# Making part of a scan's inputs on TensorE in the last layer of a four-layer network

## The chip, the cores and the metric

The kernel runs on one NeuronCore of a Trainium2 chip. The metric is the device time of one execution in microseconds, and the whole computation is in fp32. Five engines work side by side, each through its own instruction stream in order: TensorE (PE in the profile, its weight loads PEld), VectorE (DVE), ScalarE (ACT), GpSimd (POOL) and SyncE (SP), which here issues the DMAs.

## The reference

Four layers follow one another on an image batch; all of them hold selective state-space scans. Only the last one is touched. It normalises the image, runs one bidirectional Mamba over the rows and one over the columns, joins them with a linear map, and ends in an MLP. What its scans compute:

```python
def _mamba(x, W_in, conv_w, conv_b, W_x, W_dt, b_dt, A_log, D, W_out):
    xz = jnp.einsum('nld,ed->nle', x, W_in)
    xi, z = (xz[..., :di], xz[..., di:])                 # di = 384
    xp = jnp.pad(xi, ((0, 0), (K - 1, 0), (0, 0)))       # K = 4 taps
    xc = conv_b + sum((xp[:, k:k + L, :] * conv_w[:, k] for k in range(K)))
    xc = _silu(xc)
    dbc = jnp.einsum('nld,ed->nle', xc, W_x)
    dt = jax.nn.softplus(jnp.einsum('nlr,dr->nld', dbc[..., :dr], W_dt) + b_dt)
    Bm = dbc[..., dr:dr + ds]                            # ds = 16 states
    Cm = dbc[..., dr + ds:]
    A = -jnp.exp(A_log)
    def step(h, inp):
        dt_t, B_t, C_t, x_t = inp
        h = jnp.exp(dt_t[:, :, None] * A) * h + (dt_t * x_t)[:, :, None] * B_t[:, None, :]
        return (h, jnp.einsum('nds,ns->nd', h, C_t))
    ...
    y = jnp.swapaxes(ys, 0, 1) + D * xc
    y = y * _silu(z)
    return jnp.einsum('nld,od->nlo', y, W_out)

y1 = _mamba(xs, *p)
y2 = jnp.flip(_mamba(jnp.flip(xs, 1), *p), 1)            # the same weights, backwards
```

The images are 4 x 48 x 48 with 192 channels. In the last layer each row (or column) of 48 tokens is a sequence of its own.

## The kernel before

`network` runs layer 0, the inputs of layer 1, the scans of layers 1 and 2, then `row_mambas` for the last layer, then `mlp`. `row_mambas` makes a list of jobs. A job is one chunk of 384 tokens (eight sequences of 48) in one direction; the backward job of a chunk is the twin of the forward one and shares its projected input `xh` and its gate `z`. There are two sets of weights, four images, six chunks and two directions, so 96 jobs. In a job the 384 inner channels stand as three blocks `i` of 128 partitions, and the 16 states as four groups `g` of four (NG). A step of `run_jobs` handles one (job, i, g): 12 steps a job, 1152 in the layer.

In one step, VectorE (`scan`) first waits on an empty instruction for everything that the step needs, then multiplies du (delta times x, held in PSUM by `enter`) by the four rows of B, which `fetch` has spread over all partitions in `bcb`, into the PSUM tile `inputs`; then one scan instruction runs over all 4 x 384 elements with the decays `a` and writes `h`. The decay is zero at the first token of each sequence, so one scan passes over many sequences. ScalarE (`decay`) makes the four exps of a later step (`ahead` is 2), with three buffers of `a`. GpSimd (`weigh`) multiplies `h` by the four rows of C. TensorE (`reduce`) sums the states by identity matmuls into the PSUM tile `y`, which also takes D times x (`skip`, `diagD`). `take` copies `y` to SBUF on ScalarE, `gate` multiplies it by z on GpSimd. `h` has four buffers.

Beside the steps, `Stream` runs the projections of the next job as units, each with a slot in which TensorE begins it and one in which ScalarE evacuates it: `inner` (input projection), `conv` (the convolution, four matmuls with 128x128 diagonal weights `diag` for each of the three blocks), `bc` (B, C and the rank of delta; it also writes B and C to DRAM, from where `fetch` spreads them), `delta` (three of them), the z `gate` and the output projections. All of these use the two buffers of the PSUM tile `ps`. No unit is made more than two ahead of the last evacuated one. The order of a step's work on each engine is written out by hand in the loop of `run_jobs` and kept in program order on VectorE, GpSimd, TensorE and ScalarE.

[...]before, `y` takes two, `ps` two, `inputs` three and `du` one.

Of the kernel before, what the change touches and what calls it, by code (L numbers as in the profile page):

```python
# [14 lines left out]
ALU = mybir.AluOpType  # L15
# [3 lines left out]
S = 48  # L19
# [5 lines left out]
NCH = L // CH  # L25
N = 16
NG = 4

# [28 lines left out]
class K:  # L59
# [3 lines left out]
    def __init__(self, tc, ctx):  # L63
        self.tc, self.nc = tc, tc.nc
        self.v, self.g, self.t = (
            InOrder(tc, e) for e in (tc.nc.vector, tc.nc.gpsimd, tc.nc.tensor)
        )
        self.count = 0
        self.last_act = None
        self.table = None  # L70
        self.const = ctx.enter_context(tc.tile_pool(name="const", bufs=1))
        self.ident = self.tile(self.const, [128, 128], "ident")
        make_identity(self.nc, self.ident)

    def tile(self, pool, shape, tag, bufs=None):
        self.count += 1
# [161 lines left out]
class ScanPools:  # L238
# [6 lines left out]
    def __init__(self, k, ctx, parts, rows):  # L245
        pool = k.tc.tile_pool
        self.parts, self.rows = parts, rows
        self.wide = 128 // parts
        self.n = N // parts
        self.groups = self.n // NG  # L250
        self.W = W = CH if rows else CH + 1
        self.one = ctx.enter_context(pool(name="one", bufs=1))
        self.two = ctx.enter_context(pool(name="two", bufs=2))
        self.bcs = ctx.enter_context(pool(name="bcs", bufs=5 if rows else 4))
        self.hbufs = 4 if rows or parts == 2 else 3
        self.hs = ctx.enter_context(pool(name="hs", bufs=self.hbufs))
        self.y = ctx.enter_context(pool(name="y", bufs=2 if rows else 1, space=PSUM))
        self.ps = ctx.enter_context(pool(name="ps", bufs=2, space=PSUM))
        self.vec = ctx.enter_context(pool(name="vec", bufs=1, space=PSUM))

        inputs = k.tile(self.vec, [128, 1536 if rows else 2048], "inputs")
        self.b = inputs[:, : NG * W].rearrange("p (j l) -> p j l", l=W)
        self.du = k.tile(self.vec, [128, 512], "du")[:, :W]
        self.ones = k.tile(self.one, [128, 1], "ones")
        k.nc.vector.memset(self.ones, 1.0)
        self.decays = [k.tile(self.one, [128, NG, W], f"a{i}") for i in range(3)]
        self.n_decays = 0

        self.readers = []
        self.weighed = []  # L270
        self.n_h = 0
        self.entered = None
        self.revs = [None] * 3
        self.yts = 3 if rows else 2
        self.rev = None

        self.sum = k.ident
        if parts == 2:
            self.sum = k.tile(self.one, [128, 64], "sum")
            k.nc.vector.tensor_tensor(self.sum, k.ident[:, :64], k.ident[:, 64:], ALU.add)  # L280
# [28 lines left out]
class ScanJob:  # L309
# [10 lines left out]
    def close(self, i):  # L320
        pass

    def __init__(self, k, pools, w, c0, rev, prev):
        self.k, self.pools, self.w, self.c0, self.rev, self.prev = k, pools, w, c0, rev, prev
        self.entry, self.tokens = pools.entry(rev)
        self.bcb = {}
        self.fetched = {}
        self.y = {}
        self.a = {}
        self.h = {}  # L330
        self.du = {}

        self.waits = {}

# [12 lines left out]
    def projections(self, xs, *slots):  # L347

        k, nc, w, pools = self.k, self.k.nc, self.w, self.pools
        nr = 2 * N + w.rank  # L350
        W = pools.W

        def bc(px):
            self.bcd = k.tile(pools.two, [nr, W], "bcd", 1)
            if self.entry is not None:
                k.g.memset(self.bcd[:, self.entry : self.entry + 1], 0.0)
            k.copy(self.bcd[:, self.tokens], px)
            self.bc = k.dram([2 * N, W], "bc")
            nc.sync.dma_start(self.bc, self.bcd[: 2 * N, :])

        def delta(i):
            def act(pd):
                if i == 0:
                    self.delta = k.tile(pools.two, [128, 3, CH], "delta")
                k.act(self.delta[:, i, :], pd, AF.Softplus, bias=w.dtb[:, i, :])

            return self.unit(
                slots[1],
                128,
                lambda ps: (ps, [(w.dtT[2 * N : nr, i, :], self.bcd[2 * N : nr, self.tokens])]),  # L370
                act,
            )

        first = self.unit(
            slots[0],
            nr,
            lambda ps: (ps, [(w.xpT[:, i, :], xs()[: pools.wide, i, :]) for i in range(3)]),
            bc,
        )
        return first, [delta(i) for i in range(3)]  # L380

    def fetch(self, g):

# [45 lines left out]
    def enter(self, i):  # L429

        self.pools.turn(self.k, self.rev)
        self.pools.entered = self.k.copy(self.pools.du[:, self.tokens], self.du.pop(i))

    def scan(self, i, g):

# [282 lines left out]
        return units  # L718


class Stream:


# [62 lines left out]
def run_jobs(jobs, side=None):  # L786
# [1 line left out]

    ahead, behind, taken, gated, driven = 2, 1, 2, 3, 3
    last_group = jobs[0].pools.groups - 1
    groups = [(job, i, g) for job in jobs for i in range(3) for g in range(last_group + 1)]
    per = len(groups) // len(jobs)
# [14 lines left out]
    for t in range(driven):  # L809
        if first := at_group(t, 0):  # L810
            first[0].drive(first[1])
    jobs[0].enter(0)
    for job, i, g in groups[:ahead]:
        job.decay(i, g)
    stream = Stream([])
    for t in range(len(groups) + gated + 1):
        n, at = divmod(t, per)
# [5 lines left out]
        if at == per - ahead:  # L823
            stream.run(at - 1)
        if at == taken + 3 and n + 1 == len(jobs) and n:
            Stream(jobs[n - 1].outputs(*[(0, 0)] * 3)).run(per)
        if t < len(groups):
            job, i, g = groups[t]
            job.scan(i, g)
# [8 lines left out]
        if t < len(groups):  # L838
            if t + 1 < len(groups):
                job, i, g = groups[t + 1]  # L840
                job.carry(i, g)
            job, i, g = groups[t]
            job.weigh(i, g)
        stream.run(at if at < per - 1 else per)
        if t < len(groups):
            for slot, extra in jobs[n].extras:
                if slot == at:
                    extra()
# [9 lines left out]
        if 0 <= t - behind < len(groups):  # L858
            job, i, g = groups[t - behind]
            job.reduce(i, g)  # L860
    Stream(jobs[-1].outputs(*[(0, 0)] * 3)).run(per)
    offer(jobs[-1])


# [34 lines left out]
class MambaWeights(Weights):  # L899
    def __init__(self, k, pool, inT, xpT, dtT, vec, tag):  # L900
        super().__init__(k, pool, 128, 12, xpT, dtT, vec, tag)
        self.k, self.pool, self.in_src = k, pool, inT
        self.D = self.vec[:, :, 17:18]
        self.cb = self.vec[:, :, 18:19]
        self.taps = vec.shape[1] - 19
        self.diagD = k.tile(pool, [128, 3, 128], f"diagD{tag}")
        self.diag = k.tile(pool, [128, 3, self.taps, 128], f"diag{tag}")

    def scaled(self, out, by):
        self.k.nc.vector.tensor_scalar(out, self.k.ident, by, None, ALU.mult)  # L910

    def diagonals(self, i):

        self.scaled(self.diagD[:, i, :], self.D[:, i, :])
        for t in range(self.taps):
            self.scaled(self.diag[:, i, t, :], self.vec[:, i, 19 + t : 20 + t])

    def derive(self):

# [10 lines left out]
class PairWeights(MambaWeights):  # L930
# [15 lines left out]
        k.act(self.A, self.vec[:, :, 1 : 1 + N], AF.Exp)  # L946
        k.act(self.A, self.A, AF.Copy, scale=-1.0)

    def scaled(self, out, by):
        if not self.late:  # L950
            return super().scaled(out, by)
        self.k.act(out, self.k.ident, AF.Identity, scale=by)

    def extras(self):

# [632 lines left out]
def row_mambas(k, weights, sets):  # L1588
# [3 lines left out]
    with ExitStack() as ctx:  # L1592
        pools = ScanPools(k, ctx, 1, True)
        jobs = []
        for (there, back), (srcs, outs, prior) in zip(weights.pairs, sets):
            if jobs:

                jobs[-2].extras = [(1, there.enter)]
            for b in range(B):
                for c in range(NCH):  # L1600
                    of = None, srcs[b], outs[b]
                    last = prior[b] if prior is not None else None
                    first = MambaJob(k, pools, there, c * CH, False, *of)
                    jobs += [
                        first,
                        MambaJob(k, pools, back, c * CH, True, *of, twin=first, prior=last),
                    ]
        run_jobs(jobs)

# [170 lines left out]
    return np.concatenate([a if a.ndim == parts[-1].ndim else a[..., None] for a in parts], -1)  # L1780


def scan_rows(w, rank):

    bc = w[..., rank:, :]
    shape = bc.shape
    bc = bc.reshape(*shape[:-2], 2, N // NG, NG, shape[-1])
    bc = np.swapaxes(bc, -4, -3).reshape(shape)
    return swapped(np.concatenate([bc, w[..., :rank, :]], -2))


def mamba_layout(in_w, conv_w, conv_b, x_w, dt_w, dt_b, a_log, d):
    return {
        "inT": swapped(in_w),
        "xpT": scan_rows(x_w, 12),
        "dtT": swapped(dt_w),
        "vec": columns(dt_b, a_log, d, conv_b, conv_w),
    }


def layout(i):
# [50 lines left out]
    for p in ("mh", "mv"):  # L1852
        add(
            f"L3_{p}",
            **mamba_layout(
                *of(f"L3_conv_{p}", "Win", "convw", "convb", "Wx", "Wdt", "bdt", "Alog", "D")
            ),
            Wout=i[f"L3_conv_{p}_Wout"],
        )
    add(  # L1860
        "L3",
# [24 lines left out]
```

## Time and profile before

| what | value |
|---|---|
| median of 3 runs | 19325.0 us (19319.56 to 19327.51) |
| profiled execution, its own time | 19328.76 us |
| span in the profile | 19327.0 us |
| mean granted TensorE clock | 0.907 |
| VectorE busy | 18079.9 us, 94% |
| TensorE matmul busy | 16851.2 us, 87% |
| GpSimd busy | 14748.4 us, 76% |
| ScalarE busy | 13012.9 us, 67% |
| the last layer's steps | first multiply at 12872.84 us, last scan ends at 18869.98 us |

A row of the profile names a group of instructions by line, engine, operation, output and inputs, with its count, busy time, the mean of one in ns and the idle time of the engine before it. Line 56 is the helper that keeps program order, line 93 the helper of ScalarE's activations, so groups are told apart by the names of their tiles. An fp32 matmul stands as two MATMUL and two LDWEIGHTS records. A busy time of PE covers overlapping records once.

### The profile page before, as it was taken

How to read it: one execution, taken by the hardware profiler on the slowest of the kernel's cores; microseconds unless marked ns; L12 is line 12 of the kernel's file. 1: busy time of each engine (PE TensorE's matmuls, PEld its weight loads, DVE VectorE, ACT ScalarE, POOL GpSimd, SP SyncE). 2: the span in 40 equal slices, each digit the busy share in tenths (PEclk: the TensorE clock that was granted, in tenths of full speed). 3: DMA queues.
4: the chain of work that ended last, by engine and by line, in shares of the span. 5: the costliest groups of instructions: out<-in, count | busy, mean ns of one | idle time of the engine just before them, and what ended most of it. 6: DMA issues, size and time to landing. Idle time of an engine off the chain costs nothing.

```text
span 19327.0 us, 166155 instructions
## 1 busy us (share of the span) xinstructions
PE 16851.2 (87%) x49392; PEld 7999.8 (41%) x49392; DVE 18079.9 (94%) x7297; ACT 13012.9 (67%) x23158; POOL 14748.4 (76%) x10860
## 2 busy tenths in 40 slices
PE   8999999999998877787787778879999999999989
PEld 4544545444444322222222222234444444444444
DVE  9999999999998699999999999969999999999993
ACT  6766767666665467777777777766666666666663
POOL 7888888778886288888888888857777777777770
PEclk9999999999999878788887787889999999999999
DMA  3333333232332366666666666633322332333231
GB/s 114 118 112 115 122 110 127 104 117 106 117 117 90 91 142 141 151 149 152 151 150 146 141 151 148 140 110 110 107 106 104 107 112 105 109 110 112 103 107 47
DMA packets 500517, 2306.77 MB, mean 119 GB/s; under 512 B 76664, under 2 KB 334304, under 8 KB 347168
## 3 DMA queue, kind: packets, MB, share of 16 engines
q1 hardware_dynamic: 499616, 2296.14, 41.1%
q8 instruction: 396, 6.49, 0.1%
q14 instruction: 505, 4.14, 0.1%
HBM read 2103.60 MB, written 192.32 MB: 119 GB/s over the span
## 4 chain that ended last, share of the span: by engine, by line
DVE 47%; POOL 31%; PE 9%; issue 8%; ACT 3%; DMA 1%; POOLq 0%; SPq 0%; DVEq 0%; ACTq 0%
DVE h L56 30%; POOL h L56 24%; DVE inputs L56 16%; PE y L56 3%; PE ps L56 3%; POOL dus L56 2%; PE vps L128 2%; POOL state L56 1%; POOL yt L56 1%; ACT a L93 1%; PE mop L128 1%; POOL bcb L56 1%; PE mps L128 1%; DMA bcb<-bc 1%; POOL nx L56 1%
## 5 line engine op out<-in xcount | busy, mean ns | idle before, releaser
L56 POOL TENSOR_TENSOR h<-h,bcb 128x1536 f32<-128x1536 f32 x3456 | 11906.7, 3445 | 1599.4 <-DVE h L56 1137.0
L56 DVE TENSOR_TENSOR_SCAN h<-a,inputs 128x1540 f32<-128x1540 f32 (+1 forms) x3456 | 11606.4, 3358 | 145.0 <-DVE inputs L56 1.4
L93 ACT ACTIVATE a<-delta,A 128x384 f32<-128x384 f32 (+1 forms) x13824 | 7419.1, 602 | 2684.0 <-DVE h L56 2666.7
L56 PE MATMUL y<-h,ident 128*128 128x384 f32 x18432 | 6741.6, 514 | 440.9 <-POOL h L56 438.2
L56 DVE TENSOR_TENSOR inputs<-du,bcb 128x1540 f32<-128x1540 f32 (+1 forms) x3456 | 6112.5, 1769 | 419.0 <-ACT a L93 120.1
L56 PEld LDWEIGHTS y<-h,ident 128*128 128x128 f32 x18432 | 3614.9, 200 | 3410.5 <-POOL h L56 863.3
L56 PE MATMUL y<-h,sum 128*64 128x384 f32 x9216 | 2668.5, 643 | 746.0 <-POOL h L56 540.2
L56 POOL COPY state<-h 128x4 f32<-128x4 f32 x2304 | 431.5, 187 | 1950.4 <-DVE h L56 1912.0
L56 PEld LDWEIGHTS y<-h,sum 128*64 128x64 f32 x9216 | 853.6, 167 | 2175.2 <-issue 968.8
L56 PE MATMUL ps<-xh,diag 128*128 128x384 f32 x4032 | 1418.8, 491 | 171.2 <-ACT xc L93 171.0
L56 PE MATMUL ps<-bcd,dtT 12*128 12x384 f32 (+1 forms) x2304 | 1138.8, 608 | 453.0 <-ACT delta L93 449.7
L56 PE MATMUL ps<-u,inT 96*128 96x384 f32 x3456 | 1253.7, 493 | 162.2 <-ACT z L93 118.5
L56 PEld LDWEIGHTS ps<-xh,diag 128*128 128x128 f32 x4032 | 750.6, 189 | 765.9 <-ACT xc L93 259.3
L93 ACT ACT_TABLE_LOAD x794 | 1018.7, 1283 | 14.0
L90 ACT ACT_TABLE_LOAD x789 | 1012.3, 1283 | 14.2 <-PEq L1876 0.7
L56 PEld LDWEIGHTS ps<-u,inT 96*128 96x128 f32 x3456 | 650.0, 191 | 673.6 <-ACT z L93 194.8
L93 ACT ACTIVATE delta<-ps,vec 128x384 f32<-128x384 f32 x1152 | 632.2, 578 | 384.5 <-PE ps L56 379.1
L93 ACT ACTIVATE o<-ps 64x384 f32<-64x384 f32 (+1 forms) x864 | 409.2, 474 | 711.0 <-PE ps L56 711.0
L56 PEld LDWEIGHTS ps<-bcd,dtT 12*128 12x128 f32 (+1 forms) x2304 | 427.4, 213 | 1098.0 <-ACT delta L93 693.6
L56 PE MATMUL ps<-yt,outT 128*96 128x384 f32 x2304 | 789.8, 486 | 0.4 <-POOL yt L56 0.4
L93 ACT ACTIVATE du<-dus 128x384 f32<-128x384 f32 x1152 | 557.6, 484 | 141.1 <-DVE inputs L56 132.2
L56 PE MATMUL ps<-yc,sum 128*64 128x384 f32 x1152 | 643.6, 649 | 0.7 <-ACT yc L93 0.7
(133 smaller groups left out, 10570.8 us busy)
## 6 DMA issues: line engine op xcount, KB each, us to landing
bcb<-bc SPq DMA_DIRECT2D x384, 1540.0 KB
bcb<-bc SPq DMA_DIRECT2D x768, 770.0 KB
bcb<-bc SPq DMA_DIRECT2D x384, 1536.0 KB
y<-o SPq DMA_DIRECT2D x192, 288.0 KB
xs<-xi_wh SPq DMA_DIRECT2D x96, 288.0 KB
xs<-xi_hw SPq DMA_DIRECT2D x96, 288.0 KB
added<-y SPq DMA_DIRECT2D x96, 288.0 KB
xs<-x_wh SPq DMA_DIRECT2D x96, 288.0 KB
```

What stands on the lines that cost most here:

```text
L56: return lambda *a, **kw: self.tc.keep_in_program_order(op(*a, **kw))
L90: self.in_order(self.nc.scalar.preload_act_table_set(LOG_EXP))
L93: return self.in_order(self.nc.scalar.activation(out, in_, func, **kw))
L128: ins = (engine or self.nc.tensor).matmul(out, lhsT, rhs, start=start and i == 0, stop=stop and i == n - 1)
```

## The change

It touches the jobs of the last layer alone, in a new class `RowJob`; the other layers keep theirs.

- Of a group's four states, VectorE multiplies two (`given`); the products of the other two (MADE) come from TensorE. For each step `fill` makes six matmuls of 128 columns: the weights are a 128-token block of du, turned so that tokens lie on the partitions (`turn`, three transposes and a copy to `duT`), and the moving operand is a 128x128 matrix with B on its diagonal. The result goes to a PSUM tile of its own, `made_inputs`, that has one buffer.
- The diagonal matrices come from DRAM: `spread` writes the rows of B as 384 single elements each into lines of zeros that are 769 long, and `fetch` reads them back as rows of 768, which puts each element one column further. Two sets of lines alternate; they are zeroed once.
- `scan` issues one multiply of 2 x 384 elements and two scans of 2 x 384: the first on `inputs`, the second on `made_inputs`.
- `reduce` adds up the states by 12 transposes of 128x128 with the identity, so that `y` stands turned; `take` copies it, and `turn_back` turns it back on top of D times x. `behind` becomes 2 for this layer, and `taken` and `gated` follow.
- The convolution is done on 32x32 tiles (`convolved`): 32 matmuls of 192 columns for two half blocks at a time, over row groups and column groups of the array. The channels are permuted on the host to match (TURNED). The bias is added by ScalarE on evacuation; one silu covers the three blocks.
- The slots of the units move: the convolution is three units in three slots, and an output projection is split into two units.
- `y` has one buffer instead of two, `inputs` two banks instead of three, `made` takes two.

```diff
+    def spread(self):
+        n = pools.groups * (pools.given + NG)
+        self.bc = k.dram([n, CH], "bc")
+        sync.dma_start(self.bc, self.bcd[:n, :])
+        be = k.dram([pools.groups, MADE, CH], "be")
+        sync.dma_start(be.rearrange("g e l -> (g e) l"), self.bcd[n : 2 * N, :])
...
+            for e in range(MADE):
+                    sync.dma_start(
+                        line[:, :, e, 0:1], be[g, e].rearrange("(b t v) -> t b v", t=128, v=1)
+                    )
+    def turn(self, i):
+        ps = k.tile(pools.ps, [128, 512], "ps")[:, :CH]
+        self.turned_over(ps, self.du[i])
+        self.duT[i] = k.tile(pools.two, [128, CH], "duT")
+        k.copy(self.duT[i], ps)
+    def fill(self, i, g):
+        for b in range(3):
+            at = slice(b * 128, (b + 1) * 128)
+            for e in range(MADE):
+                k.t.matmul(
+                    pools.made_inputs[:, e * CH : (e + 1) * CH][:, at],
+                    self.duT[i][:, at],
+                    self.bcb[g][2][:, b, e, :],
+                    start=True,
+                    stop=True,
+                    skip_group_check=True,
+                )
+    def scan(self, i, g):
...
+        n = pools.given
+        du = pools.du.unsqueeze(1).to_broadcast([128, n, CH])
+        k.v.tensor_tensor(pools.b, du, self.bcb[g][0], ALU.mult)
...
+        for at, b in (
+            (slice(0, n), pools.b.rearrange("p j l -> p (j l)")),
+            (slice(n, NG), pools.made_inputs),
+        ):
+            k.v.tensor_tensor_scan(
+                h[:, at, :].rearrange("p j l -> p (j l)")[:, ::step],
+                a[:, at, :].rearrange("p j l -> p (j l)")[:, ::step],
+                b[:, ::step],
+                0.0,
+                ALU.mult,
+                ALU.add,
+            )
+    def reduce(self, i, g):
...
+        for j in range(NG):
+            for b in range(3):
+                at = slice(b * 128, (b + 1) * 128)
+                ins = k.t.matmul(
+                    self.y[i][:, at],
+                    h[:, j, at],
+                    k.ident,
+                    start=g + j + b == 0,
+                    stop=g == pools.groups - 1 and j == NG - 1,
+                    is_transpose=True,
+                    skip_group_check=True,
+                )
+    def turn_back(self, i):
+        back = k.tile(self.pools.ps, [128, 512], "ps")[:, :CH]
+        k.t.matmul(back, self.w.diagD[:, i, :], self.xs[:, i, :], start=True, stop=False, skip_group_check=True)
+        self.turned_over(back, self.turned, False)
...
+        k.copy(self.yt[:, i, :], back)
+    def convolved(self, step, *slots):
+        both = [(n % 3, n // 3) for n in (2 * step, 2 * step + 1)]
...
+            made.extend(k.tile(pools.ps, [128, 512], "ps")[:, :HALF] for _ in both)
+            for t, off in enumerate(offs):
+                for r in range(4):
+                    rows = slice(r * 32, (r + 1) * 32)
+                    for (i, n), ps in zip(both, made):
+                        c = (r + i) % 4
+                        x = self.xh[rows, i, n * RC // 2 : (n + 1) * RC // 2, off : off + S]
+                        k.t.matmul(
+                            self.shaped(ps[c * 32 : (c + 1) * 32]),
+                            w.diag[rows, i, t, :],
+                            x,
+                            start=t == 0,
+                            stop=t == w.taps - 1,
+                        )
...
+                k.act(self.xs[:, i, at], ps, AF.Identity, bias=w.cb[:, i, :])
+            if step == 2:
+                k.act(self.xs, self.xs, AF.Silu)
...
-    ahead, behind, taken, gated, driven = 2, 1, 2, 3, 3
+    behind = 2 if jobs[0].pools.rows else 1
+    ahead, taken, gated, driven = 2, behind + 1, behind + 2, 3
...
+        if back := at_group(t - gated, last_group):
+            back[0].turn_back(back[1])
         stream.run(at if at < per - 1 else per)
+        if soon := at_group(t + 2, 0):
+            soon[0].turn(soon[1])
...
             job.reduce(i, g)
+        if t + 1 < len(groups):
+            job, i, g = groups[t + 1]
+            job.fill(i, g)
```

The slots after the change: a forward job has `inner` in slots 0 to 2, `convolved` in 3 to 5, `bc` in 6, the deltas in 8 and the z gates in 9 to 11; a twin has `convolved` in 0 to 2, `bc` in 4, the deltas in 6 and the output units in 7 to 11.

## The prediction

> **What bounds the kernel now.** I read the page first, then the groups of the stretch in which the last layer runs, then TensorE's timeline over a few steps. From the page, busy time by engine, granted clock in 40 slices, and the chain of waits by engine:
>
> ```profile
> PE 16851.2 (87%) x49392; PEld 7999.8 (41%) x49392; DVE 18079.9 (94%) x7297; ACT 13012.9 (67%) x23158; POOL 14748.4 (76%) x10860
> ...
> PEclk9999999999999878788887787889999999999999
> ...
> DVE 47%; POOL 31%; PE 9%; issue 8%; ACT 3%; DMA 1%; POOLq 0%; SPq 0%; DVEq 0%; ACTq 0%
> ```
>
> VectorE is busy 94% of the span. Only the last layer's row scans change: 96 jobs of 12 steps, 1152 steps, from 12873 us to 18870 us. The groups of that stretch (busy us, mean ns, idle time before them and its cause):
>
> ```profile
> L56 DVE TENSOR_TENSOR_SCAN h<-a,inputs 128x1536 f32<-128x1536 f32 x1147 | 3846.0, 3353 | 59.5 <-DVE inputs L56 1.4
> L56 DVE TENSOR_TENSOR inputs<-du,bcb 128x1536 f32<-128x1536 f32 x1147 | 2025.6, 1766 | 39.6
> ...
> L56 POOL TENSOR_TENSOR h<-h,bcb 128x1536 f32<-128x1536 f32 x1148 | 3956.6, 3447 | 1391.7 <-DVE h L56 1115.6 <-issue 208.7 <-PE ps L56 55.7
> ...
> L56 PE MATMUL y<-h,ident 128*128 128x384 f32 x9185 | 3372.8, 517 | 302.4 <-POOL h L56 301.9
> L56 PE MATMUL ps<-xh,diag 128*128 128x384 f32 x2256 | 788.4, 491 | 40.6 <-ACT xc L93 40.3
> ...
> L56 PE MATMUL ps<-bcd,dtT 12*128 12x384 f32 x570 | 275.7, 594 | 160.2 <-ACT delta L93 160.2
> ```
>
> See that VectorE's two instructions have almost no idle time: 1.766 + 3.353 us and 0.07 of gaps make the step of **5.19 us**, and POOL, ACT and TensorE wait for it. Busy time in that stretch (columns: us, PE, PEld, DVE, ACT, POOL, clock, DMA share, GB/s):
>
> ```profile
> 12910.87:18880.00 5969.13, 5448.99 (x15392) 2900.13 (x15391) 5860.19 (x2290) 3907.91 (x6741) 4576.56 (x2309) 0.95 0.30 107
> ```
>
> TensorE is second. An fp32 product stands as two passes; eight passes of 384 columns take 2.74 us, so 0.32 us a pass at full clock. The timeline shows what happens when it runs dry:
>
> ```profile
> 16015.82 2.85 PE L56 MATMUL y<-h,ident 128*128 128x384 f32 x8
> 16020.92 4.54 PE L56 MATMUL y<-h,ident 128*128 128x384 f32 x8 [2.25 <-POOL h L56]
> 16025.39 1.55 PE L56 MATMUL ps<-bcd,dtT 12*128 12x384 f32 x4
> 16027.93 1.63 PE L56 MATMUL ps<-bcd,dtT 12*128 12x384 f32 x2 [0.99 <-ACT delta L93]
> ```
>
> After 2.25 us of idling the same eight passes take 4.54 us: half clock.
>
> [...]half-clock records last 3.413 or 6.827 us. Weighting each matmul's streaming time by rows times columns over 128x128, I count in the records: of 878 windows under 0.28 of a full one, 837 were followed by half clock; of 628 between 0.28 and 0.40, 216; of 4124 above, none. [...]the 64-column sums of the middle layers start 6 ns apart[...]
>
> **VectorE, part by part.** The multiply shrinks to 768 elements. A PSUM-operand multiply of 96x768 in the last stage takes 0.949 us, so 0.95. The scan becomes two of 768: 1540 against 1536 elements differ by 8 ns, so 2.08 ns an element and 0.153 fixed: 1.75 us each. Gaps: 0.10 after the multiply and 0.03 after a scan, as now. 0.95 + 3.50 + 0.16 = **4.62 us**, 0.57 less. With nothing else in the way that is 1152 x 0.57 = 657 us.
>
> **TensorE, per step at full clock.** Removed: the sum over states, 8 x 0.32 = 2.56, and the convolution, 24 passes a job, 0.64 a step. Added:
> - `fill`: six products of 128 columns, 12 passes. The 192-column passes that make outT start 0.163 apart when warm, 0.320 cold (streaming plus 3 ns); a 128-column load occupies 0.107 (the second of a pair starts that much after the first). So 0.11 a pass, 1.31 us. Bounds 0.11 to 0.19, the loads' whole duration.
> - the sums: 12 transposes. [...]upper 0.218 (two passes like a product). [...]I take 0.07: 0.84 us.
> - turning du and y: 18 transposes a job, 0.10 a step; diagD stays, 0.16.
> - the convolution: three units a job, 64 passes of 192 columns over eight tiles. With all eight beside each other 8 x 0.16 = 1.28 us; only four row groups at once, 2.6; serial, 10. I take 1.5 and 0.2[...]: 0.43 a step.
> - unchanged: inT 0.32, outT 0.32, dtT 0.16, xpT 0.16.
>
> Sum 3.80, and some 0.4 for four restarts a step (0.10 of load before a first pass): 4.2 against VectorE's 4.62, where before it was 4.3 against 5.19. TensorE fits, barely.
>
> **The new wait.** `made_inputs` has one buffer. `fill` of the next step waits for the second scan of this one, and the next second scan waits for `fill`. Between them lie the multiply and first scan, 0.95 + 0.10 + 1.75 = 2.8 with its gap; `fill` needs 1.31 + 0.10 load + 0.16 drain (a pass's 0.48 duration less 0.32) + 0.1 semaphore = 1.67. So TensorE may reach it 1.1 us late before VectorE stalls. Queued behind the waiting `fill` on TensorE: the units, the turns, the sums, hence POOL's buffers, and ACT's evacuations.
>
> Where TensorE is later: (a) the step of the three deltas. Two `ps` buffers, so the third waits for the first to be evacuated, behind four exps (2.11), a table load (1.28) and the softplus (0.58): 3.97 us into the step. Then the product 0.64, sums 1.0, fill 1.67: 7.3, just what is allowed (4.62 + 2.8). But TensorE has idled and dtT has 12 rows, so the clock halves, as at 16027.93; sums and fill then cost about 2.3 more. I charge 2.5 us a job. (b) steps where `turn_back` precedes a unit: the unit needs the buffer that ACT frees after its exps (2.6); 2.6 + 1.7 + 1.0 + 1.67 = 7.0 fits warm, not at half clock. Three a job, 0.55 each: 1.7. Job: 12 x 4.62 + 4.2 = 59.6 us against 62.3, a step of 4.97.
>
> **What costs nothing, and its cover.** POOL keeps its work: 4577 us over 1150 steps, 3.98 a step, 0.64 spare; uncovered it would set 4.1. ACT gains three duT copies, three yT copies and six 192-column copies for three (0.48 and, as outT, 0.33: 4.9 us a job), a 1152-wide silu (1.2, at 0.8 ns a column) for three at 0.58, and loses up to four table loads of 1.28: even; 3.4 of 4.62 a step, and if the loads stay 3.8. SP: per job one more write and eight scatters of 384 four-byte elements, 0.40 each by the like weight load, so 4 us of issue and about 2 to land; twice the fetches. The block for group 0 was fetched 37 us ahead of use; landing takes 5.3 us and DMA is 30% busy, so they hide; late, a 5 us stall a job. h is held one step longer (`behind` 2) within four buffers. Once: zeroing the lines, 3.1 MB, 10 us.
>
> **Sum.** 96 x 2.7 = 260, less 10 for the start, is 250 off the profiled execution's 19328.8 us (span 19327.0): 19079. The median of the runs is 4 lower, so 19080 within rounding.
>
> **Rivals.**
> 1. *VectorE alone decides*: [...]tiles fully parallel, no clock loss. Step 4.62 to 4.75: 18670 to 18830. [...]Against: the deltas' wait. Chance 0.13.
> 2. *TensorE's clock becomes the bound, slower.* Place: every step's sums and light units. Full-array streaming a step now: 2.56 + 0.64 + 0.70 = 3.9 of 5.19, 0.75 of a window. After: fill 1.28, convolution 0.16 (a sixteenth of the array each), the rest 0.70, transposes 0 to 0.64: 2.1 to 2.8 of 4.97, 0.43 to 0.56, near the 0.28 to 0.40 where half clock begins. If a third to half of the time is at half clock, 4.2 becomes 5.5 to 6.2: 357 to 1160 us more, 19680 to 20490. It decides from a mean step of 5.19, stalls of 6.9 us a job instead of 4.2; transposes at 0.11 or tiles four at a time would also get there. Chance 0.31.
> 3. *Gain and stalls cancel*, 5.15 to 5.23: 19280 to 19370. Chance 0.08.
> 4. *The tiles do not run beside each other* (the change doesn't do what it says): three units of 10 us add 2.1 us a step; 5.9 or more, 20150. Chance 0.03.
>
> The forecast case has 0.45; its own range is 18850 to 19250.
>
> **Numbers.** Faster by over 0.2% (about 39 us, what a measurement of this kernel can tell from no change): rival 1 and the forecast, with a part of rival 3, 0.60; within: 0.07; slower: rivals 2 and 4, 0.33. The range leaves a tenth at each end: below 18720 lies only the bare VectorE floor, above 19900 the heavier half of rival 2.
>
> **What would show it.** Right: multiply near 0.95, scans near 1.75; VectorE's idle time before the second scan put down to TensorE `made`, about 0.35 us a step; transposes 0.06 to 0.08 apart; clock in the last layer 0.85 to 0.92. Wrong: clock under 0.82 or TensorE busy over 95% (rival 2); VectorE over 97% busy (rival 1); waits for the fetched diagonals or SP.

## The result and the profile after

The changed kernel takes 19115.85 us (median of 4 runs, 19112.1 to 19121.62) against 19324.99 us (19319.56 to 19327.51): ratio 0.9892, 95% interval 0.9875 to 0.991. The forecast was 19080 us. The time is close to it by luck: two errors in the sum nearly cancel, and the reason given is only half right. I predicted VectorE as the bound with TensorE fitting barely beside it. TensorE sets the pace, by its work and by what it waits for, and about three quarters of what VectorE saves (895 us of busy time, against 235 us of length) is lost to it.

The last layer runs from the first multiply at 12893.7 us to the end of the last scan at 18656.0 us, 5762 us instead of 5997. All of the gain is there; the rest takes some 22 us more in these two traces, which is within the scatter of the kernels below that leave that rest alone (13325 to 13355 us). Lines 59 and 104 are now the helpers that were 56 and 93. From the page of after (engine lines, granted clock by slice):

```profile
PE 16743.5 (88%) x85680; PEld 9426.4 (49%) x85680; DVE 17183.8 (90%) x8452; ACT 13342.8 (70%) x24116; POOL 14745.6 (77%) x10861
...
PEclk9999999999999977888777788789999999999999
```

VectorE went from 94% to 90% of a shorter span, and the clock of the last layer (from slice 27 on) did not fall. The busy time of the layer, of before and then of after (us, then PE, PEld, DVE, ACT, POOL, clock, DMA share, GB/s):

```profile
12873.00:18870.00 5997.00, 5469.61 (x15443) 2910.50 (x15442) 5897.13 (x2304) 3937.02 (x6789) 4595.83 (x2315) 0.95 0.30 107
```
```profile
12893.00:18656.00 5763.00, 5322.34 (x51559) 4319.14 (x51559) 5001.90 (x3456) 4264.54 (x7742) 4591.78 (x2314) 0.98 0.37 113
```

TensorE is busy for 5322 of 5763 us, 4.62 us a step, VectorE for 5002. Before, VectorE had 5897 of 5997. The groups of that stretch (busy, mean ns, idle time before and its cause):

```profile
L59 DVE TENSOR_TENSOR_SCAN h<-a,inputs 128x768 f32<-128x768 f32 x1152 | 2020.2, 1754 | 60.8 <-DVE inputs L59 1.4
L59 DVE TENSOR_TENSOR_SCAN h<-a,made 128x768 f32<-128x768 f32 x1152 | 2005.3, 1741 | 637.6 <-PE made L59 637.1
L59 DVE TENSOR_TENSOR inputs<-du,bcb 128x768 f32<-128x768 f32 x1152 | 1107.7, 962 | 104.9 <-ACT du L104 61.8 <-ACT a L104 43.1
```
```profile
L59 PE MATMUL made<-bcb,duT 128*128 128x128 f32 x13824 | 1797.7, 281 | 113.3 <-DVE h L59 110.2 <-ACT a L104 3.0
L59 PE MATMUL y<-ident,h 128*128 128x128 f32 x13824 | 1787.1, 281 | 58.3 <-ACT yT L104 55.6 <-POOL h L59 2.7
L59 PE MATMUL ps<-xh,diag 32*32 32x192 f32 x18240 | 468.8, 324 | 8.7 <-issue 2.0
...
L59 PE MATMUL ps<-ident,dus 128*128 128x128 f32 x861 | 170.5, 311 | 206.2 <-POOL dus L59 199.3 <-ACT xc L104 6.6
```

VectorE's one new wait stands where it was forecast: 637 us ahead of the second scan, put down to `made`. TensorE's own largest wait, the last line, was not: it stands at `turn`, waiting for `dus`, which is delta times x, so du itself, made by GpSimd in `drive` (the expectations below that call it du*B, or a product of du and B, mean this). The timeline shows both ends, TensorE's lines and then GpSimd's (start us, duration us):

```profile
15999.69 1.55 PE L59 MATMUL ps<-xh,diag 32*32 32x192 f32 x64
16001.98 0.55 PE L59 MATMUL ps<-ident,dus 128*128 128x128 f32 x3 [0.75 <-POOL dus L59]
16002.37 1.47 PE L59 MATMUL y<-ident,h 128*128 128x128 f32 x12
16003.68 1.50 PE L59 MATMUL made<-bcb,duT 128*128 128x128 f32 x12
...
16020.48 0.91 PE L59 MATMUL ps<-bcd,dtT 12*128 12x384 f32 x2 [0.38 <-ACT delta L104]
16021.55 0.90 PE L59 MATMUL ps<-ident,dus 128*128 128x128 f32 x3 [0.16 <-POOL dus L59]
16022.24 2.77 PE L59 MATMUL y<-ident,h 128*128 128x128 f32 x12
```
```profile
15997.52 3.46 POOL L59 TENSOR_TENSOR h<-h,bcb 128x1536 f32<-128x1536 f32 x1 [0.93 <-POOL h L59]
16000.93 0.99 POOL L59 TENSOR_TENSOR dus<-delta,xc 128x384 f32<-128x384 f32 x1
```

GpSimd's `dus` waits its turn behind the 3.46 us product of `weigh`; at 16001.92 it ends, 0.06 us later `turn` starts, and only then come the sums and the fill for which VectorE is waiting. The costliest place of this kind is slot 3 of the twin, where `dus` stands behind two products of `weigh`, TensorE idles for 2.82 us, then runs at half clock (granted clock 0.51 from 16063.13 to 16065.89), and VectorE idles for 3.58 us:

```profile
16054.57 6.86 POOL L59 TENSOR_TENSOR h<-h,bcb 128x1536 f32<-128x1536 f32 x2
16061.37 1.01 POOL L59 TENSOR_TENSOR dus<-delta,xc 128x384 f32<-128x384 f32 x1
```
```profile
16062.44 0.90 PE L59 MATMUL ps<-ident,dus 128*128 128x128 f32 x3 [2.82 <-POOL dus L59]
16063.13 2.76 PE L59 MATMUL y<-ident,h 128*128 128x128 f32 x12
```
```profile
16067.31 1.75 DVE L59 TENSOR_TENSOR_SCAN h<-a,made 128x768 f32<-128x768 f32 x1 [3.58 <-PE made L59]
```

At 16002.37 the sums' twelve transposes start 1.31 us ahead of the fill, so they are 0.109 us apart.

Cut at VectorE's multiplies, the trace gives the length of each of a job's 12 steps (slots 0 to 11). A step without a wait takes 4.32 us from multiply to multiply, so a job could take 51.8. A forward job takes 59.26 on average and its twin 60.90 (62.47 before; first and last pair left out): 16.5 us lost per pair. Slots 3, 7 and 11, each right after a `turn`, lose 10.7 of it by the means (9.2 by the medians, which the first expectation below quotes). A `turn` is not all that stands ahead of them: a job's steps run the units of the next job, so slot 6 of the forward job also has the three deltas of the twin. Experiment e2 sorts these places.

### The profile page after: what moved, and what is told of

It is laid out like the page before. It is cut to its first block, busy times and chain, and to the rows that moved or that the text cites. A ratio compares the mean times of both kernels' runs of the same rounds, so it can differ in the third digit from the quotient of the medians.

```text
span 19114.8 us, 243541 instructions
## 1 busy us (share of the span) xinstructions
PE 16743.5 (88%) x85680; PEld 9426.4 (49%) x85680; DVE 17183.8 (90%) x8452; ACT 13342.8 (70%) x24116; POOL 14745.6 (77%) x10861
## 5 line engine op out<-in xcount | busy, mean ns | idle before, releaser
L59 DVE TENSOR_TENSOR_SCAN h<-a,inputs 128x1540 f32<-128x1540 f32 (+1 forms) x3456 | 9764.1, 2825 | 146.7 <-DVE inputs L59 2.3
L59 DVE TENSOR_TENSOR inputs<-du,bcb 128x1540 f32<-128x1540 f32 (+1 forms) x3456 | 5185.7, 1500 | 463.2 <-ACT a L104 119.8
L59 PE MATMUL y<-h,ident 128*128 128x384 f32 x9216 | 3362.8, 511 | 131.0 <-POOL h L59 129.0
L59 PEld LDWEIGHTS y<-h,ident 128*128 128x128 f32 x9216 | 1796.3, 199 | 1605.0 <-POOL h L59 315.0
L59 DVE TENSOR_TENSOR_SCAN h<-a,made 128x768 f32<-128x768 f32 x1152 | 2005.3, 1741 | 637.6 <-PE made L59 637.1
L59 PE MATMUL made<-bcb,duT 128*128 128x128 f32 x13824 | 1797.7, 281 | 113.3 <-DVE h L59 110.2
L59 PE MATMUL y<-ident,h 128*128 128x128 f32 x13824 | 1787.1, 281 | 58.3 <-ACT yT L104 55.6
L59 PEld LDWEIGHTS made<-bcb,duT 128*128 128x128 f32 x13824 | 1682.7, 197 | 161.6 <-DVE h L59 157.5
L59 PEld LDWEIGHTS y<-ident,h 128*128 128x128 f32 x13824 | 1601.1, 145 | 305.3 <-issue 155.6
L59 PE MATMUL ps<-xh,diag 32*32 32x192 f32 (+1 forms) x20160 | 1088.7, 339 | 140.7 <-ACT xc L104 131.7
```

What stands on the lines that cost most here:

```text
L59: return lambda *a, **kw: self.tc.keep_in_program_order(op(*a, **kw))
```

## The experiments

The table gives, for the last layer of each profiled run, its length, TensorE's busy time and the rest in which it has no matmul running, and VectorE's busy time. The time is the median of the kernel's runs, the ratio is to runs of before on the same occasion. Outside that layer all kernels but e11 take 13325 to 13355 us.

| kernel | time, us | ratio to before (interval) | layer, us | TensorE busy | TensorE idle | VectorE busy |
|---|---|---|---|---|---|---|
| before | 19325 | 1 | 5997 | 5470 | 527 | 5897 |
| after | 19116 | 0.9892 (0.9875 to 0.991) | 5763 | 5322 | 441 | 5002 |
| e1 turn late | 19209 | 0.9951 (0.9934 to 0.9967) | 5884 | 5312 | 572 | 4978 |
| e2 drive early | 18934 | 0.9803 (0.9788 to 0.9817) | 5594 | 5308 | 286 | 4993 |
| e3 plain sums | 19985 | 1.0343 (1.0327 to 1.0358) | 6630 | 6542 | 88 | 5038 |
| e6 fill out | 18609 | 0.9626 (0.961 to 0.9642) | 5270 | 4032 | 1238 | 4957 |
| e9 drive early, silu apart | 18839 | 0.9746 (0.9731 to 0.976) | 5501 | 5264 | 237 | 4995 |
| e11 take first | 19455 | 1.0065 (1.005 to 1.008) | 5609 | 5305 | 304 | 4998 |
| e12 e9 with fill out | 18433 | 0.9542 (0.9528 to 0.9556) | 5082 | 4025 | 1057 | 4943 |
| e13 no fill, VectorE makes all | 19342 | 1.0014 (1.0007 to 1.0021) | 5997 | 4245 | 1752 | 5897 |

### e1: turn behind the sums and the fill

```diff
-        if soon := at_group(t + 2, 0):
-            soon[0].turn(soon[1])
 ...
             job.fill(i, g)
+        if soon := at_group(t + 2, 0):
+            soon[0].turn(soon[1])
```

> The step's call of turn (the three transposes of du*B and its copy) goes from ahead of reduce and fill to behind them. Theory A (mine after reading the trace of after): VectorE's idle time ahead of the second scan, 16.5 us per pair of jobs and 9.2 of it in the three steps right after a turn, is TensorE standing at turn's transposes until POOL's drive has made their input, with the sums and the fill of the next step queued behind. It expects 6 to 9 us less for each of 48 pairs: 18690 to 18830 us. Theory B (the prediction's): the stalls are the step in which the deltas are made and the turn back ahead of each unit, which this edit does not touch: 19060 to 19115 us. Theory C: TensorE, busy for 92% of the layer, is the bound and the waits are only where its lateness shows: 19080 to 19150 us.

Slower than after by 93 us, and outside the ranges of all three theories. The waits of the layer:

```profile
POOL h L59 <- DVE h L59: 1162.7, 650, 16.2
ACT duT L104 <- PE ps L59: 647.6, 239, 4.8
DVE h L59 <- PE made L59: 453.5, 190, 4.4
DVE inputs L59 <- ACT du L104: 386.9, 237, 2.4
```

VectorE's wait for `made` did fall, from 637 to 454 us, but ScalarE now stands for 648 us (185 in after) at the copy of the turned du, which comes out of TensorE later. Behind that copy in ScalarE's order is the copy that enters du into PSUM, and VectorE's multiply waits for it, 387 us instead of 62. The edit moved the wait from TensorE to ScalarE's queue. It does not decide where the 16.5 us a pair came from.

### e2: drive one step earlier

```diff
-    ahead, taken, gated, driven = 2, behind + 1, behind + 2, 3
+    ahead, taken, gated = 2, behind + 1, behind + 2
+    driven = 4 if jobs[0].pools.rows else 3
```

> In the last layer drive (POOL's product of du and B) is issued four steps ahead instead of three, so that the input of turn is made a step earlier; turn stays where it is. Theory A (turn waits for POOL): the wait goes with it, 18690 to 18850 us. Theory B (deltas and turn back are the stalls) and theory C (TensorE is the bound): 19075 to 19155 us, about no change.

182 us less than after: in the direction of theory A, but 84 us short of its range, and clearly outside that of B and C. The layer lost 169 us and TensorE's idle time 155. The layer's line, and the one of the second scan:

```profile
12886.00:18480.00 5594.00, 5308.12 (x51556) 4320.61 (x51557) 4992.79 (x3456) 4261.77 (x7742) 4594.25 (x2314) 0.98 0.38 116
```
```profile
L59 DVE TENSOR_TENSOR_SCAN h<-a,made 128x768 f32<-128x768 f32 x1152 | 2003.2, 1739 | 472.8 <-PE made L59 472.7
```

No wait of TensorE for `dus` is left among the 24 largest of the layer. By jobs, only the twin became shorter, 60.90 to 57.12 us; the forward job stayed, 59.26 to 59.66. The loss per pair fell from 16.5 to 13.1 us: about a fifth of it was GpSimd's place in the order, which the prediction did not have. Sorted by what stands ahead of a step on TensorE, VectorE waits for `made` (us for each pair of jobs):

| slots of the waiting steps | ahead of them on TensorE | after | e2 |
|---|---|---|---|
| 3 and 11 of both jobs | a `turn` | 4.3 | 1.2 |
| 7 of the forward job, 9 of the twin | the deltas of the next job (with a `turn` in the first) | 2.9 | 3.5 |
| 0 and 8 of the forward job, 4 of the twin | a turn back | 3.0 | 2.0 |
| 7 of the twin | a `turn`, and sums that wait 1.16 us for ScalarE to copy the last sum out of `y`, which has one buffer | 2.7 | 2.6 |
| others | | 0.4 | 0.5 |

So the edit took the wait away where it was aimed at, and the waits after the deltas and at `y` stayed.

### e3: the sums by identity matmuls, as before

```diff
 class RowJob(MambaJob):
-    def reduce(self, i, g): ...
-    def take(self, i): ...
-    def turn_back(self, i): ...
```

> The sums over the states are made as in the kernel before, by four matmuls of 384 columns with the identity for each step, without the turn of the sum and the turn back. Each has 384 columns[...], so TensorE has about 1.1 us more in each of 1152 steps of 5.0 us. If TensorE's time is what the last layer's length is made of (92% busy): up to 20040 us. If there is slack of 1.1 us as the prediction has it: stalls in the steps with units and deltas alone, 19200 to 19460 us.

```profile
12886.00:19516.00 6630.00, 6542.31 (x46085) 4408.63 (x46070) 5037.65 (x3456) 4174.66 (x7453) 4586.49 (x2314) 0.99 0.33 98
```

TensorE's busy time rises by 1220 us (1.06 a step, as expected), the layer by 867, and TensorE's idle time falls from 441 to 88 us: 1220 - 353 = 867. TensorE is busy for 98.7% of the layer and sets its length. The time, 19985 us, is what the expectation gave if TensorE's work makes the length. (The trace has two passes of 0.32 us to a matmul, so 2.56 us for the sums against 1.31.) The 1.1 us of the prediction is how late one fill may be, not time that TensorE has free in every step; of that its own sum had 0.4, and 0.38 were there. So the core of theory C (TensorE is the bound) holds, but not the conclusion that its waits cost nothing, which e2 refutes: the layer is TensorE's work plus what TensorE waits.

Of the parts, the tiled convolution should have been undone in the same way (e4, full diagonals of 128 rows as before; up to 290 us more were expected if TensorE's time sets the length). That version did not fit into the memory: its buffers of `h` need 24 kb per partition, and 17.3 were left. So there is no time for it.

### e6: the fill left out

```diff
-        if t + 1 < len(groups):
-            job, i, g = groups[t + 1]
-            job.fill(i, g)
```

> The loop's fill is left out, so only the first step's products of the two states are made and the second scan of every later step reads those (the products of all later steps are left out of the computation); all other work stays. TensorE is rid of 12 passes in 1.5 us in each of 1151 steps, from 4.62 us of busy time per step to about 3.1. Theory C2 (mine after the first runs: TensorE's own work of 4.62 us per step, and not VectorE's 4.32, is what the length of the last layer is made of, with 4 us of waiting per job on top): VectorE becomes the bound, 4.35 to 4.50 us per step, 18350 to 18520 us. The prediction's account (VectorE bound at 4.97 with stalls in two places that the fill does not cause): 18900 to 19100 us. On the clock: if transposes count as activity, the half-clock share of the last layer stays under 5%; if they do not, most of TensorE's counted work is gone with the fill, the half clock takes over a third of the layer, and the time is above 18700 us.

18609 us, 507 under after, yet above the range of the theory, whose direction holds. A step takes 4.575 us. VectorE no longer waits for `made` at all, but 208 us for du; TensorE waits 560 us for `dus` and 356 for the deltas. The half clock held for 21% of the layer (granted clock 0.89), between the two expectations; see the last section. The run takes away the fill's work and the waits for the one buffer of `made` together.

### e9: drive early and the twin's silu apart

The 128x1152 silu of the convolved rows (1.16 us) stood in ScalarE's order, with table loads of 1.28 us, ahead of the copy that enters du; in the forward job VectorE waited 1.3 us for it at slot 4. The edit of e2, and:

```diff
+    def late_silu(self, *slots):
+        return slots, lambda: None, lambda: self.k.act(self.xs, self.xs, AF.Silu)
...
-            if step == 2:
+            if step == 2 and self.twin is None:
...
+                self.late_silu(3, 3),
```

> drive four steps ahead, and the second job's silu of the convolved rows (1.16 us on ACT, 128x1152) as a unit of its own in slot 3, away from the step in which du is entered. Theory: with drive early, half of what TensorE still waits for comes from VectorE's 1.4 us idle ahead of one multiply per pair (it waits for ACT's du behind that silu), after which TensorE waits 1.9 us for the scan. With that gone 1.4 to 1.9 us per pair go, 48 pairs: 67 to 91 us below the kernel with drive early alone (18934 us), 18843 to 18867 us. If TensorE's work is the only limit and its waits are made up elsewhere: 18920 to 18935 us.

18839 us, 95 less than e2, just under the range. The wait for du has gone from the multiply's line (67 us in e2):

```profile
L59 DVE TENSOR_TENSOR inputs<-du,bcb 128x768 f32<-128x768 f32 x1152 | 1108.3, 962 | 41.1 <-ACT a L104 41.1
```

This is the fastest version that computes everything. TensorE is busy for 96% of its layer.

### e11: take ahead of the decays

The edits of e9, and:

```diff
+        if done := at_group(t - taken, last_group):
+            done[0].take(done[1])
         coming = at_group(t + 1, 0)
...
-        if done := at_group(t - taken, last_group):
-            done[0].take(done[1])
```

> As the one with drive early and the silu apart, and ACT's take of a finished sum (the copy out of the PSUM tile that the next sum is transposed into) goes ahead of the decays of its step, not behind them. TensorE waits 1.16 us per pair there, ahead of the first transpose of a new sum. If that wait goes and nothing new comes: 56 us less than that kernel, some 18800 us. If the decays, now 0.5 us later, become late for VectorE's scans: no change or slower by up to 70 us.

A loss of 616 us against e9, of which only 108 us are in the last layer: the loop is shared, and the other layers, which the edit reached as well, lost about 510 us. The 108 us are more than the 70 that the second expectation allowed. In the last layer ScalarE stands at that copy:

```profile
ACT yT L104 <- PE y L59: 405.3, 240, 3.4
```

The sum is finished late by TensorE, so an earlier copy stops ScalarE with the decays behind it. TensorE's 1.16 us wait at slot 7 of the twin is gone, and VectorE's wait there fell from 2.6 to 1.3 us; but two slots later it rose from 1.3 to 2.5, and four slots later from nothing to 1.6.

### e12: e9 with the fill left out

Edit: e9's and e6's together.

> As the kernel with drive early and the silu apart, and the loop's fill left out besides (the products of two states in all steps but the first are left out of the computation). Asked: what the 0.25 us per step above VectorE's own 4.32 us were, which stayed when the fill alone was left out (18609 us, 4.575 us per step). Theory: they were VectorE's wait for du and TensorE's for POOL's du*B, which the two moves take away: 4.36 to 4.45 us per step, 18350 to 18470 us. If they were the half clock, which held for 21% of the layer there and stays: 18560 to 18620 us.

```profile
12865.00:17947.00 5082.00, 4025.07 (x37754) 2905.02 (x37755) 4942.55 (x3456) 4250.42 (x7741) 4583.08 (x2315) 0.91 0.41 128
```

18433 us, 4.41 us a step: the theory's range. VectorE is busy for 97% of the layer, while 18% of it is still at half clock, which can cost no more than the 3% that are left. This is close to what VectorE alone allows. e9 stands 406 us above it; that is the price of the fill, its work on TensorE and the waits for its one buffer together. In e9 TensorE itself waits 53 us for a scan to free that buffer; what a second one would bring was not tried.

### e13: the change without its main part

```diff
-MADE = 2
+MADE = 0
...
     def turn(self, i):
-        ...
+        pass
     def fill(self, i, g):
-        ...
+        pass
```

`scan` has one instruction over 1536 elements again, and the diagonals and their transfers are gone.

> The change without its main part: VectorE multiplies du*B of all four states and scans them in one instruction, as before, and turn, fill, the diagonals and their transfers are gone; the transposed sums, the tiled convolutions, the spread units and the order of the loop stay. TensorE then has about 3.0 us per step. Theory A (the time comes from VectorE's shorter step alone, and the other parts only make room on TensorE): a step as before, 5.13 to 5.21 us, 19240 to 19335 us. Theory B (the other parts bring time themselves): below 19220 us.

```profile
12893.00:18890.00 5997.00, 4244.91 (x36813) 2983.07 (x36814) 5897.35 (x2304) 4138.55 (x7454) 4600.23 (x2314) 0.83 0.30 107
```

Theory A: the layer is as long as before to the microsecond, with VectorE's busy time the same, although TensorE works 1225 us less than before and its clock fell to 0.83. The whole run, 19342 us, is 7 us above the range of the theory and 0.14% above before; that lies outside the layer. As long as VectorE's step is the old one, transposed sums, tiled convolutions and spread units bring no time. e3 shows what at least the sums are for: with plain ones the change is 3.4% slower than before. What the tiled convolution is worth stays open.

## Why the prediction was right, and where not

**The total** was 36 us off, and that is luck: VectorE's step was put 346 us too long in all, and the stalls some 385 us too short (4.0 us in each of 96 jobs).

- *VectorE's step: 4.62 forecast, 4.32 measured.* The durations were right (0.962, 1.754 and 1.741 against 0.95 and 1.75). The term that failed is the gaps, 0.16 forecast. That was too much for before already: the idle time that the prediction shows ahead of the two instructions is 0.05 and 0.03 us a step. In the records of after there are +0.05 us on average ahead of the first scan, which reads the multiply's result, and -0.08 ahead of both the second scan and the next multiply: these start before the recorded end of the instruction ahead of them. Neither reads what that one writes. I had carried over the gaps of before, where every instruction used the buffer of the one ahead; none of those gaps is under 0.03 us. 1152 x 0.30 = 346 us too much.
- *TensorE's step: 4.2 forecast, 4.62 measured busy.* The term that failed is the transposes, put at 0.07 us, which no trace of before showed, and far below the upper bound of 0.218. They start 0.109 apart, the same as the fill's passes (1.31 us for 12 against 1.34). The sums are 1.31 instead of 0.84, and the 18 that turn du and y 0.18 a step instead of 0.10 (0.39 and 0.33 for three). Fill was right at 1.31, and the convolution was near: 64 passes in 1.55 us for a unit that I put at 1.7. That makes the sum of passes about 4.3 instead of 3.80, an estimate from these spacings. The comparison with before was uneven, too: the 4.2 has 0.4 for restarts in it, the 4.3 of before has not; the prediction's own line, 5449 us of busy time, gives 4.75 a step there.
- *The bound.* With both corrected, TensorE's 4.62 stands above VectorE's 4.32. "VectorE bound, TensorE fits, barely" was the wrong way round; e3 shows it, and e12 shows that VectorE alone would allow 4.41.
- *The stalls: 4.2 us a job forecast, 8.2 measured* (60.1 less 51.8). The two places that I named are there, the deltas also in the way described: TensorE has idled, the clock halves, and the sums take 2.77 us instead of 1.47 (at 16022.24, with a granted clock of 0.52); nearly 2 us of half clock a job stand in these slots, and VectorE waits 1.7 and 1.2 us there, for which I charged 2.5 a job. After a turn back it waits 3.0 us a pair, for which I charged 3.4. What I left out is the rest. I had listed `turn` only by its cost on TensorE and not asked who makes its input. It takes GpSimd's `dus`, which is queued behind a 3.46 us product; e2 shows that this was worth 182 us. And `y` has one buffer, for whose copy by ScalarE TensorE waits in slot 7 of the twin; e11 moved that copy, and the kernel became slower.
- *The covers.* GpSimd stayed under the step (4592 of 5763 us). ScalarE was not even: 4265 against 3937 us, since no table load was lost (568 in the layer against 570; 3.70 us a step, where I had 3.8 if the loads stay), and the silu and its loads stood ahead of du, 95 us by e9 against e2. No wait for the diagonals or SP is among the layer's large ones.

**The rivals.** Rival 2, TensorE as the bound through the clock, had the right engine and the wrong cause: the clock of the layer rose from 0.95 to 0.98, and forecast 0.85 to 0.92 was wrong too. Its remark that transposes at 0.11 would also bring a step over 5.19 was wrong: they did take 0.109, and the step is 5.00. Rival 1's time, 18670 to 18830, is near what e9 reaches with two moves. Rivals 3 and 4 fell: the tiles do run beside each other, and the gain did not cancel.

**The signs.** Multiply, scans and the wait for `made` were as listed (0.55 us a step, not 0.35); the spacing of the transposes and the clock were not. The sign for TensorE as the bound, busy for over 95%, did not show either: it was 92%, because an engine that sets the pace can still wait.

## What to carry to other kernels

When work moves from the bound engine to the second one, add up both steps with equal care: here 0.04 us more on each transpose, with 0.3 us less on VectorE's step, changed the bound. For every instruction that is put ahead of others in an in-order queue, ask who makes its input and what is ahead of that in its maker's queue; here producing the input one step earlier was worth nearly as much (182 us) as the whole change (209 us). Moving the waiting instruction back (e1) or an evacuation forward (e11) only moved the wait to the next queue.

## What the runs showed of the hardware that was not expected

- *Transposes appear to count as activity for the clock.* Stretches at half clock are not only of 3.413 and 6.827 us, as the prediction read: the trace of before has 302 and 160 of these, and also 77 of 10.24 and 28 of 13.65. Cut into windows of 3.413 us along these records, with matmuls weighted as in the prediction (0.32 us for 384 columns, times the share of the array), the last layer of before, which has no transposes, has 130 windows under 0.28, all followed by half clock, and 1563 above 0.40, none followed by it. In the layer of after, if transposes weigh nothing, 344 windows are under 0.28 and 73 were followed by half clock. If they weigh fully, 65 are and 48 were, and above 0.40 none of 1542. Counting them as nothing does not fit these two traces. How much they count is not shown: at full weight 48 of 65 is not yet 130 of 130. It is a reading of records; e6's share of half clock, 21%, fell between what its two expectations said, so it did not settle the question by itself. The twelve transposes at 16022.24 took 2.77 us at a granted clock of 0.52, against 1.47 at 1.00 (at 16002.37): they slow down with the clock too.
- *A transpose of 128x128 in fp32 took one pass:* 0.109 us from start to start, where a 128-column fp32 product of the fill takes two passes of 0.112. The gain over a product was a factor of two here. The weight load of a transpose takes 145 ns by the records; whether it sets the spacing was not tried.
- *Eight 32x32 tiles ran largely beside each other:* 64 passes of 192 columns in 1.55 us (at 15999.69, with a granted clock of 1.00), 24 ns a pass with 324 ns of recorded duration each. By the prediction's sum all eight side by side would take 1.28 us, four at a time 2.6.
